# A six-product offset convolution in a deformable-convolution kernel, with the next image's tables begun one band earlier

## The chip, the cores and the metric

One NeuronCore of a Trainium2 chip runs the whole program. The metric is device time in microseconds (us). The kernel before took 1505.65 us, the median of three runs.

## The reference

Two layers work on eight images of 128 channels by 64 by 64 pixels, all float32. In layer 0 each image is group-normalised (32 groups), a 3x3 convolution makes 27 offset-and-mask maps from it, and a deformable 3x3 convolution samples the normalised image at those offsets. Its output is batch-normalised over all images, passed through a relu and added to the input. Layer 1 group-normalises the result and adds a mixture of four 3x3 convolutions (the two best per image, weighted) and a shared one.

```python
om = conv(gn(x), off_w, 3x3, pad 1) + off_b          # 27 maps: 9 (dy, dx) pairs, 9 masks
py, px = row + dy + ky - 1, column + dx + kx - 1      # for each of 9 taps
val = bilinear(gn(x), py, px) * sigmoid(mask)
y = einsum('bckhw,ock->bohw', val, w) + b
x = x + relu(batchnorm(y) * gamma + beta)
x = x + sum_e w_e * conv_e(gn(x)) + conv_shared(gn(x)) + biases
```

## The kernel before, in words

Layer 0 is the function `dense` and takes the first 1127.6 us of the profile; layer 1 takes the rest. `dense` is written with a manual schedule: every engine executes its instructions in the order in which the Python code emits them. So the order of the code is the order of each queue.

The work is cut into 64 **bands**, eight for each image, of eight image rows each. Band `g` belongs to image `b` and has the place `j` (0 to 7) in it. For each band the main loop emits, in this order:

- five **samples** (`sample`, line 714): matmuls of transposed pixels `xt` with bilinear weights `s` into the PSUM tile `pq` (three buffers). ScalarE moves each `pq` into `samples` (line 724). VectorE makes the `s` (`weights`, line 698) three samples ahead, from two weight tables `xwts` and `ywts`.
- nine **taps** of the deformable convolution of the band before (`conv`, line 763) into `py` (one PSUM buffer), which ScalarE moves out as `y` (line 771). In band 0 of an image the taps number eighteen, because the last band of the image before is cut into two pieces.
- among the taps: four groups of transposes `pt` (line 672) which ScalarE copies out as `xt` (line 677), the absolute values and clamps of `xwts` (lines 648 on ScalarE, 650 on VectorE), and copies of the pixels of a later band (`picked`, line 657).

`pt`, and every other PSUM tile of the offset work (`pm`, `pv`, `pc`), share **one** PSUM buffer (pool `ps_c`). A matmul into one of them waits until the one before it has been read.

The **tables** of an image are its bilinear weights. They are made from its offset convolution by a generator `tables(b)`, which `tick()` advances by one `yield` several times after each tap; `pause(n)` is n empty yields, so it sets how many ticks later the next piece is emitted. A `yield BLOCK` holds the generator until a tap whose number is in `BLOCKS`. The tables of image b+2 are begun in band 7 of image b and finished in band 5 of image b+1, just ahead of the first `load_x` for image b+2. The steps for one image are:

1. `statistics` (line 294): eight `bn_stats` on VectorE and one aggregate `mv`; six of them are emitted in band 6, the last two and the aggregate in band 7.
2. `pm` and `pv` (lines 309, 319): two one-column matmuls that average over a group's channels, in band 7 after the third and fourth tap. VectorE makes `d`, `e`, `gm` between them and `ve` after; GpSimd raises `ve` to the power -1/2 (`scale`, line 325), and VectorE makes `shift`.
3. The normalisation in place of `pad` in eight chunks, four on ScalarE (line 332) and four on VectorE (line 336).
4. The offset convolution. It takes rows in pairs: four **products** j = 0 to 3, each over half the rows. VectorE makes the row combinations `combo` (`combine`, line 360, two instructions of 128x1024 each), TensorE multiplies (`tap`, line 379: 3 column taps by 4 row groups of 32 PSUM partitions, 512 columns each), and VectorE adds the product into `om` (lines 408 to 415; ScalarE starts `om` at line 402).
5. ScalarE turns `om` (line 422), SyncE's queue writes it to DRAM (`rowwise`, `colwise`, lines 427 and 432) and reads it back with pixels on the partitions (lines 465 and 452). VectorE prepares distances from it (lines 503 to 518), the x table is stored (line 483), ScalarE makes five `tent`s of two instructions each (lines 537 and 541), VectorE multiplies each by the mask (line 574), and the y table is stored (line 564).

GpSimd's queue loads the tables: each band emits `load_x` for three bands ahead (line 632, two DMAs) and `load_y` for two bands ahead (line 617, eight DMAs). Image quarters are loaded by SyncE's queue in bands 2 to 5 (`load_quarter`, line 272).

## Time and profile before

| what | us |
|---|---|
| median of 3 runs (1500.36 to 1507.43) | 1505.65 |
| the profiled execution | 1504.96 |
| its span | 1503.2 |
| TensorE busy in the span | 1363.5 |
| VectorE busy | 959.3 |
| ScalarE busy | 818.3 |
| GpSimd busy | 449.9 |
| images 0 to 7 of layer 0, each from its first sample to the next image's | 147.5, 129.7, 133.2, 129.5, 129.3, 136.2, 128.2, 123.6 |

The image times count from the first sample matmul of band 0 of one image to that of the next, in the trace; image 0 starts at 70.5 us, and image 7 ends with the last tap of the deformable convolution at 1127.6 us. Image 7 makes no tables, so its bands show what a band costs without them.

### The profile page before, as it was taken

How to read it: one execution, taken by the hardware profiler on the slowest of the kernel's cores; microseconds unless marked ns; L12 is line 12 of the kernel's file. 1: busy time of each engine (PE TensorE's matmuls, PEld its weight loads, DVE VectorE, ACT ScalarE, POOL GpSimd, SP SyncE). 2: the span in 40 equal slices, each digit the busy share in tenths (PEclk: the TensorE clock that was granted, in tenths of full speed). 3: DMA queues.
4: the chain of work that ended last, by engine and by line, in shares of the span. 5: the costliest groups of instructions: out<-in, count | busy, mean ns of one | idle time of the engine just before them, and what ended most of it. 6: DMA issues, size and time to landing. Idle time of an engine off the chain costs nothing.

```text
span 1503.2 us, 21231 instructions
## 1 busy us (share of the span) xinstructions
PE 1363.5 (91%) x7714; PEld 761.6 (51%) x7714; DVE 959.3 (64%) x1906; ACT 818.3 (54%) x1095; POOL 449.9 (30%) x745
## 2 busy tenths in 40 slices
PE   4279799999999999999999899999994999999998
PEld 1245465556555555555556555566551444444443
DVE  5555475576557657656764775554528887888882
ACT  2365674776577468658656865866634232322320
POOL 6333242443334244333423333343303010110100
PEclk9589899999999999999999999999996999999999
DMA  4486775986697498669748866788708345665411
GB/s 143 115 181 126 175 163 105 213 190 137 128 202 179 95 196 214 137 130 207 187 99 183 194 147 135 168 183 200 171 26 248 93 124 149 168 168 154 110 45 58
DMA packets 130939, 227.27 MB, mean 151 GB/s; under 512 B 82003, under 2 KB 88303, under 8 KB 122137
## 3 DMA queue, kind: packets, MB, share of 16 engines
q0 software_dynamic: 54960, 137.08, 43.9%
q1 hardware_dynamic: 74848, 88.25, 19.9%
q8 instruction: 63, 1.03, 0.3%
q10 hardware_dynamic: 1017, 0.50, 0.1%
q14 instruction: 51, 0.42, 0.1%
HBM read 180.23 MB, written 45.35 MB: 150 GB/s over the span
## 4 chain that ended last, share of the span: by engine, by line
PE 53%; DMA 12%; ACT 9%; issue 9%; DVE 7%; SPq 2%; POOL 1%; ACTq 0%; DVEq 0%; POOLq 0%
PE py L763 20%; PE pc L1414 12%; PE pq L714 11%; PE pc L379 5%; PE pt L672 4%; DMA xwts<-tabx 4%; DMA pad<-in_x_dram 2%; ACT xwts L648 2%; ACT xt L677 2%; DMA combo<-colwise 2%; ACT work L537 1%; DMA x<-in_x_dram 1%; DMA yd<-y 1%; ACT samples L724 1%; DMA combo<-rowwise 1%
## 5 line engine op out<-in xcount | busy, mean ns | idle before, releaser
L763 PE MATMUL py<-samples,dw_sb 128*128 128x512 f32 (+3 forms) x1296 | 577.3, 562 | 7.1 <-ACT y L771 5.3
L617 POOL DMA_DIRECT2D ywts<-taby x504 | 305.5, 624 | 279.6 <-DMA xwts<-tabx 228.3
L714 PE MATMUL pq<-s,xt 64*128 64x144 f32 (+1 forms) x3840 | 283.8, 301 | 35.8 <-DVE s L698 24.7
L714 PEld LDWEIGHTS pq<-s,xt 64*128 64x128 f32 x3840 | 257.6, 190 | 84.7 <-ACT samples L724 24.2
L724 ACT COPY samples<-pq 128x864 f32<-128x864 f32 (+1 forms) x320 | 280.7, 974 | 33.6 <-PE pq L714 33.3
L763 PEld LDWEIGHTS py<-samples,dw_sb 128*128 128x128 f32 x1296 | 217.1, 190 | 160.3 <-issue 133.3
L677 ACT COPY xt<-pt 128x512 f32<-128x512 f32 (+1 forms) x256 | 142.4, 556 | 209.7 <-PE pt L672 209.2
L698 DVE TENSOR_TENSOR s<-xwts,ywts 128x72 f32<-128x72 f32 (+1 forms) x447 | 199.4, 499 | 84.6 <-PE pq L714 43.6
L650 DVE TENSOR_SCALAR xwts<-xwts 128x1152 f32<-128x1152 f32 (+2 forms) x130 | 97.3, 749 | 186.6 <-ACT xwts L648 186.2
L672 PEld LDWEIGHTS pt<-ident,picked 128*128 128x128 f32 x960 | 110.9, 141 | 171.7 <-ACT xt L677 105.0
L1414 PE MATMUL pc<-v,u 128*128 128x512 f32 x384 | 175.8, 605 | 6.3 <-DVE v L1321 6.3
L672 PE MATMUL pt<-ident,picked 128*128 128x128 f32 x960 | 152.8, 279 | 29.6 <-ACT xt L677 27.1
L632 POOL DMA_DIRECT2D xwts<-tabx x128 | 72.8, 573 | 353.5 <-DVE s L698 276.8
L1414 PE MATMUL pc<-v,wmix 128*128 128x512 f32 x384 | 174.0, 598 | 0.0
L648 ACT ACTIVATE xwts<-xwts,place 128x1152 f32<-128x1152 f32 (+2 forms) x130 | 160.9, 1242 | 11.5 <-DMA xwts<-tabx 11.5
L1392 ACT ACTIVATE t<-pc,bmix 128x512 f32<-128x512 f32 x32 | 22.0, 687 | 189.2 <-PE pc L1414 100.5
L1414 PEld LDWEIGHTS pc<-v,u 128*128 128x128 f32 x384 | 72.7, 192 | 93.5 <-issue 84.7
L1414 PEld LDWEIGHTS pc<-v,wmix 128*128 128x128 f32 x384 | 72.3, 190 | 91.4 <-issue 89.6
L360 DVE TENSOR_TENSOR combo<-pad 128x1024 f32<-128x1024 f32 x61 | 73.3, 1229 | 23.0 <-PE pc L379 14.4
L657 DVE COPY picked<-pad 128x960 f32<-128x960 f32 x128 | 81.9, 681 | 0.0
L771 ACT ACTIVATE y<-py,db_sb 128x512 f32<-128x512 f32 (+3 forms) x72 | 45.7, 635 | 65.6 <-PE py L763 31.1
L837 DVE BATCH_NORM_STATS2 ystats<-y 128x6 f32<-128x512 f32 (+3 forms) x72 | 44.5, 626 | 21.0 <-ACT y L771 21.0
(173 smaller groups left out, 955.3 us busy)
## 6 DMA issues: line engine op xcount, KB each, us to landing
xwts<-tabx POOLq DMA_DIRECT2D x128, 576.0 KB, 7.6
ywts<-taby POOLq DMA_DIRECT2D x504, 90.0 KB, 8.1
pad<-in_x_dram SPq DMA_DIRECT2D x36, 512.0 KB
out_dram<-yo SPq DMA_DIRECT2D x32, 512.0 KB
yd<-y SPq DMA_DIRECT2D x48, 256.0 KB
pad<-yd SPq DMA_DIRECT2D x16, 512.0 KB
x<-yd SPq DMA_DIRECT2D x16, 512.0 KB
x<-in_x_dram POOLq DMA_DIRECT2D x16, 512.0 KB, 9.2
```

The source lines that it names most:

```text
L379: nc.tensor.matmul(pcs[j][32 * q : 32 * q + 32].rearrange("p (h w) -> p h w", w=W)[:, :, lo:hi], lhsT=weight_of[j][:, kx], rhs=combo_of[j] ...
L617: engine.dma_start(out=y_wts[g % 2][at : at + NR * Q, r].rearrange("p a b c -> p (a b c)"), in_=bass.AP(tensor=y_table[b].tensor, offset=y ...
L648: nc.scalar.activation(part, part, AF.Abs, bias=column)
L650: nc.vector.tensor_scalar(part, part, -1.0, 0.0, ALU.add, ALU.min)
L657: nc.vector.tensor_copy(picked[g % 2][:, :, h], bass.AP(tensor=one.tensor, offset=one.offset, ap=[list(one.ap[0]), [T, NCOL], [W, Q], [1, Q]],
L672: nc.tensor.transpose(pt[:, c], picked[g % 2][:, c0 + c].rearrange("p h y x -> p (h y x)"), ident,)
L677: nc.scalar.copy(xts[g][:, c0 : c0 + n], pt[:, 0:n])
L698: engine.tensor_tensor(s[:, :, 3 * at : 3 * (at + k)].rearrange("p m (c x) -> p m c x", x=3), by_x[:, :, c : c + k], by_y[:, :, w : w + k] ...
L714: nc.tensor.matmul(by_m[:, h, :, at : at + k], lhsT=xts[g][rows, c], rhs=s[rows, :, at : at + k], start=True, stop=True,)
L724: nc.scalar.copy(bass.AP(tensor=one.tensor, offset=one.offset + first, ap=[list(one.ap[0]), [M * PLANE, 2], [PLANE, M], [WB + 1, 3], [1, w ...
L763: nc.tensor.matmul(py, lhsT=dw_sb[:, 3 * (2 - yy) + 2 - xx], rhs=samples[g % 2][:, m : m + 3 * n - 2 : 3, xx, 1 : W + 1], start=(i == 0), ...
L1414: nc.tensor.matmul(pc, lhsT=us[j][:, kx], rhs=vs[g][:, rows, kx : kx + W], start=(kx == 0), stop=(kx == 2),)
```

## The change

From the third image on (b = 2 to 7) the offset convolution takes rows in fours instead of pairs, with **six** products over a quarter of the rows each in place of four over half of them. Two products of 256 columns each go into one PSUM tile (`pair`), so there are three blocks in place of four. The row combinations are `combine_pair` (four VectorE instructions for each of three pairs); ScalarE moves every product from PSUM into SBUF, and VectorE combines them there (`mix`). The six weight sets are made once, in band 5 of image 0 (`quad_weights`).

The order moves too. All eight `bn_stats` are emitted in band 6, two after each of four taps, and `pm` and `pv` follow the eighth and ninth tap of band 6 (`BLOCKS` gets an 8). A tick at the very start of band 7 emits the power on GpSimd before that band's loads. Pauses before `shift`, before the combinations and after the loads of `om` change. Four small tiles of layer 1 get one buffer instead of two.

```diff
@@ tables(b) @@
                 ve = small.tile([P, 1], F32, name="ve")
+                if b > 1:
+                    yield
                 nc.vector.tensor_scalar(ve, pv[:, 0:1], GN_EPS, None, ALU.add)
-                yield from pause(3)
+                yield from pause(3 if b < 2 else 1)
                 scale = small.tile([P, 1], F32, name="scale")
                 nc.gpsimd.tensor_tensor(scale, ve, nhalf, ALU.pow)
-                yield from pause(8)
+                yield from pause(8 if b < 2 else 4)
...
+                def mix(out, a, times, c):
+                    if times in (1, -1):
+                        op = ALU.add if times == 1 else ALU.subtract
+                        nc.vector.tensor_tensor(out, c, a, op)
+                    else:
+                        nc.vector.scalar_tensor_tensor(out, a, float(times), c, ALU.mult, ALU.add)
+                def combine_pair(n):
+                    lo, hi = halves[n % 2]
+                    for args in (
+                        ((lo, row(2), -4, row(4)), (hi, row(1), -4, row(3)),
+                         (lo, hi, 1, lo), (hi, hi, -2, lo)),
+                        ((lo, row(2), -1, row(4)), (hi, row(1), -1, row(3)),
+                         (lo, hi, 2, lo), (hi, hi, -4, lo)),
+                        ((lo, row(2), -1.25, row(0)), (lo, row(4), 0.25, lo),
+                         (hi, row(3), -5, row(5)), (hi, row(1), 4, hi)),
+                    )[n]:
+                        mix(*args)
+                        yield from pause(PACE[n])
+                def pair(n):
+                    yield BLOCK
+                    pc = ps_c.tile([P, CH], F32, name="pc", tag="pc")
+                    for i, j in enumerate(((1, 2), (3, 4), (0, 5))[n]):
+                        weight = quad_of[j]
+                        for kx in (1, 0, 2):
+                            lo, hi = max(0, 1 - kx), min(W, W + 1 - kx)
+                            for q in range(4):
+                                nc.tensor.matmul(
+                                    pc[32 * q : 32 * q + 32, CH // 2 * i : CH // 2 * (i + 1)]
+                                    .rearrange("p (h w) -> p h w", w=W)[:, :, lo:hi],
+                                    lhsT=weight[:, kx],
+                                    rhs=halves[n % 2][i][
+                                        :, 4 * q : 4 * q + 4, lo + kx - 1 : hi + kx - 1],
+                                    start=(kx == 1), stop=(kx == 2), skip_group_check=True)
+                    pcs[n] = pc.rearrange("p (i t w) -> p i t w", i=2, w=W)
+                    yield from pause(2)
+                if b < 2:
...
+                else:
+                    yield from pause(11)
+                    yield from combine_pair(0)
+                    yield from combine_pair(1)
+                    yield from pair(0)
+                    nc.scalar.activation(quad[:, 0], pcs[0][:, 0], AF.Identity, bias=offb_sb)
+                    nc.scalar.copy(quad[:, 1], pcs[0][:, 1])
+                    yield from pause(4)
+                    mix(quad[:, 0], quad[:, 1], 1, quad[:, 0])
+                    mix(quad[:, 1], quad[:, 1], -2, quad[:, 0])
+                    yield from combine_pair(2)
+                    yield from pair(1)
+                    nc.scalar.copy(quad[:, 2:4], pcs[1])
+                    yield
+                    yield from pair(2)
+                    ends = om[:, 1, 0:CH].rearrange("p (i t w) -> p i t w", i=2, w=W)
+                    nc.scalar.copy(ends, pcs[2])
+                    for at, a, times, c in (
+                        (2, 3, 1, 2), (3, 3, -2, 2),
+                        (0, 2, 1, 0), (2, 2, 3, 0), (1, 3, 2, 1), (3, 3, 6, 1),
+                    ):
+                        mix(quad[:, at], quad[:, a], times, quad[:, c])
+                    mix(quad[:, 0], ends[:, 0], 1, quad[:, 0])
+                    mix(quad[:, 3], ends[:, 1], 1, quad[:, 3])
+                    yield
...
-                yield from pause(50)
+                yield from pause(50 if b < 2 else 57)
@@ main loop @@
-            PIXELS, BLOCKS, SPREAD = (0, 1, 5, 6), (2, 3, 4, 7), (1, 3, 5, 7)
+            PIXELS, BLOCKS, SPREAD = (0, 1, 5, 6), (2, 3, 4, 7, 8), (1, 3, 5, 7)
+            def quad_weights():
+                v0, v1, v2, v3, v4, v5 = quad_of
+                nc.vector.tensor_tensor(v2, v0, v5, ALU.add)
+                nc.vector.tensor_tensor(v1, v2, v3, ALU.add)
+                nc.vector.tensor_tensor(v2, v2, v3, ALU.subtract)
+                nc.vector.scalar_tensor_tensor(v4, v5, 4.0, v0, ALU.mult, ALU.add)
+                nc.vector.scalar_tensor_tensor(v3, v3, 2.0, v4, ALU.mult, ALU.add)
+                nc.vector.scalar_tensor_tensor(v4, v4, 2.0, v3, ALU.mult, ALU.subtract)
+                for v, n in ((v1, -6.0), (v2, -6.0), (v3, 24.0), (v4, 24.0)):
+                    nc.scalar.activation(v, v, AF.Copy, scale=1.0 / n)
...
                 turned = pixels(g + 1) if g + 1 < len(bands) else iter(())
+                if j == NB - 1:
+                    tick()
...
-                    if odd == 0 and (j == NB - 2 and part < 6 or j == NB - 1 and part < 2):
-                        next(means_of, None)
-                    if odd == 0 and j == NB - 1 and part == 2 and b + 2 < B:
+                    if odd == 0 and j == NB - 2 and part in (0, 1, 2, 4):
+                        for _ in range(2):
+                            next(means_of, None)
+                    if odd == 0 and j == NB - 2 and part == 7 and b + 2 < B:
                         made = tables(b + 2)
                         next(made)
...
+                if g == 5:
+                    quad_weights()
```

The tiles `yscale`, `yshift`, `tot` and `mb` of layer 1 change from two buffers to one (`bufs=1`).

More of the change, by code (lines that the diff above doesn't have):

```diff
@@ L199, in dense @@
             offu_sb = [a1.tile([P, 3, 32], F32, name=f"offu_sb{i}") for i in range(2)]
+            offv_sb = a1.tile([P, 3, 32], F32, name="offv_sb")
+            quad_of = (
+                offw_sb[:, 0:3], offu_sb[0], offu_sb[1], offw_sb[:, 3:6], offv_sb, offw_sb[:, 6:9]
+            )
             offb_sb = a1.tile([P, 1], F32, name="offb_sb")
@@ L397, in block @@
                     yield from pause(2)
-                for j in (1, 2):
-                    yield from combine(j)
-                yield from block(1)
-                nc.scalar.activation(even, taken(1), AF.Identity, bias=offb_sb)
-                yield from combine(0)
-                yield from block(2)
-                if b == 0:
-                    yield from combine(3)
-                m2 = taken(2)
-                nc.vector.tensor_tensor(odd, even, m2, ALU.subtract)
-                nc.vector.tensor_tensor(even, even, m2, ALU.add)
@@ L410, in tables, with row @@
-                if b:
-                    yield from combine(3)
-                yield from block(0)
-                nc.vector.tensor_tensor(even, even, taken(0), ALU.add)
-                yield from block(3)
-                nc.vector.tensor_tensor(odd, odd, taken(3), ALU.subtract)
-                yield
+                PACE = 2, 2, 2
+                quad = omr.rearrange("p (t i w) -> p i t w", i=4, w=W)
+                halves = [(t[:, 0 : H // 4], t[:, H // 4 :]) for t in combos]
+                def row(k):
+                    return pad[:, ROWPAD - 1 + k :][:, 0 : H - 3 : 4]
@@ new lines, in mix @@
+                def mix(out, a, times, c):
[7 more added lines that the diff above has]
+                    for args in (
+                        (
+                            (lo, row(2), -4, row(4)), (hi, row(1), -4, row(3)),
+                            (lo, hi, 1, lo), (hi, hi, -2, lo),
+                        ),
+                        (
+                            (lo, row(2), -1, row(4)), (hi, row(1), -1, row(3)),
+                            (lo, hi, 2, lo), (hi, hi, -4, lo),
+                        ),
+                        (
+                            (lo, row(2), -1.25, row(0)), (lo, row(4), 0.25, lo),
+                            (hi, row(3), -5, row(5)), (hi, row(1), 4, hi),
+                        ),
+                    )[n]:
+                        mix(*args)
+                        yield from pause(PACE[n])
@@ new lines, in pair @@
+                def pair(n):
[11 more added lines that the diff above has]
+                                    rhs=halves[n % 2][i][
+                                        :, 4 * q : 4 * q + 4, lo + kx - 1 : hi + kx - 1
+                                    ],
+                                    start=(kx == 1), stop=(kx == 2),
+                                    skip_group_check=True,
+                                )
+                    pcs[n] = pc.rearrange("p (i t w) -> p i t w", i=2, w=W)
+                    yield from pause(2)
@@ new lines, in tables @@
+                if b < 2:
+                    for j in (1, 2):
+                        yield from combine(j)
+                    yield from block(1)
+                    nc.scalar.activation(even, taken(1), AF.Identity, bias=offb_sb)
+                    yield from combine(0)
+                    yield from block(2)
+                    if b == 0:
+                        yield from combine(3)
+                    m2 = taken(2)
+                    nc.vector.tensor_tensor(odd, even, m2, ALU.subtract)
+                    nc.vector.tensor_tensor(even, even, m2, ALU.add)
+                    if b:
+                        yield from combine(3)
+                    yield from block(0)
+                    nc.vector.tensor_tensor(even, even, taken(0), ALU.add)
+                    yield from block(3)
+                    nc.vector.tensor_tensor(odd, odd, taken(3), ALU.subtract)
+                    yield
[23 more added lines that the diff above has]
+                    mix(quad[:, 3], ends[:, 1], 1, quad[:, 3])
+                    yield
@@ L1134, in layer1 @@
     def layer1():
-        yscale = small.tile([P, 1], F32, name="yscale")
+        yscale = small.tile([P, 1], F32, name="yscale", bufs=1)
         rsqrt(yscale, ymv[:, 1:2], BN_EPS)
         nc.vector.tensor_tensor(yscale, yscale, gamma_sb, ALU.mult)
-        yshift = small.tile([P, 1], F32, name="yshift")
+        yshift = small.tile([P, 1], F32, name="yshift", bufs=1)
         nc.vector.tensor_tensor(yshift, ymv[:, 0:1], yscale, ALU.mult)
@@ L1299, in prepare @@
                 )
-                tot = small.tile([P, 1], F32, name="tot")
+                tot = small.tile([P, 1], F32, name="tot", bufs=1)
                 nc.vector.tensor_reduce(tot, wd, AX.X, ALU.add)
@@ L1306, in mix_biases @@
                 def mix_biases():
-                    mb = small.tile([P, NE], F32, name="mb")
+                    mb = small.tile([P, NE], F32, name="mb", bufs=1)
                     nc.vector.tensor_tensor(mb, eb_sb, wd, ALU.mult)
```

## The prediction, made before the changed kernel ran

> **What bounds the kernel now.** I read the page first (busy times, then the chain that ended last), then the table by stretches with one stretch for each band of image 3, then TensorE's timeline inside those bands.

> ```profile
> PE 1363.5 (91%) x7714; PEld 761.6 (51%) x7714; DVE 959.3 (64%) x1906; ACT 818.3 (54%) x1095; POOL 449.9 (30%) x745
> ```

> ```profile
> 480.80:500.90 20.10, 18.41 (x136) 12.54 (x135) 14.58 (x25) 13.12 (x18) 5.82 (x10) 1.00 0.58 118
> 500.90:523.10 22.20, 21.99 (x166) 10.55 (x165) 13.31 (x25) 9.32 (x13) 5.64 (x10) 1.00 0.44 93
> 523.10:537.20 14.10, 14.10 (x94) 8.57 (x93) 8.61 (x18) 10.98 (x14) 6.19 (x10) 1.00 0.82 173
> ...
> 565.20:581.10 15.90, 14.47 (x95) 8.57 (x94) 10.18 (x21) 15.47 (x24) 5.71 (x9) 1.00 0.81 193
> 581.10:595.00 13.90, 13.90 (x94) 8.50 (x93) 11.95 (x24) 9.98 (x14) 7.02 (x10) 1.00 0.99 241
> 595.00:610.30 15.30, 14.63 (x98) 8.83 (x97) 9.31 (x24) 9.69 (x13) 7.17 (x13) 1.00 0.78 179
> ```

> The columns are stretch, length, then busy us (count) of PE, PEld, DVE, ACT and POOL. TensorE is busy 14.0 of 14.0 us in a plain band: it is the bound, at full clock. Image 7 makes no tables; its bands 0 and 1 take 15.9 and 13.6. So an image costs 15.9 + 13.6 + 6 x 14.0 = 113.5 without tables, and image 3, at 129.5, pays 16.0 for them: bands 0, 1, 5 and 7 hold it. What stands in them is this:

> ```profile
> 638.09 2.83 PE L379 MATMUL pc<-combo,offu_sb 128*32 128x512 f32 x24
> 613.88 1.93 PE L714 MATMUL pq<-s,xt 64*128 64x144 f32 x24 [0.93 <-ACT samples L724]
> 568.50 1.93 PE L714 MATMUL pq<-s,xt 64*128 64x144 f32 x24 [0.66 <-ACT samples L724]
> 578.87 0.55 PE L672 MATMUL pt<-ident,picked 128*128 128x128 f32 x3 [0.77 <-ACT xt L677]
> 603.69 0.35 PE L309 MATMUL pm<-mv,gsel 128*128 128x1 f32 x2 [0.67 <-DVE mv L297]
> ```

> One product takes about 2.75 us, four take 11.0. The rest are waits: 0.93 in band 0 (ScalarE late by three normalisations of 0.7), 0.66 and 0.77 in band 5 (ScalarE late by the tents), 0.67 in band 7 (VectorE's statistics). In the same view images 2 and 5 lose 2.95 and 4.51 more in band 5 waiting for `s`, whose tables came late, and image 2 2.12 at `pm`; that is why they take 133.2 and 136.2.

> [...]

> **The change, part by part** (one image, unless said).

> *Products.* 512 columns cost 423 ns a round of four, so 256 should cost about 212 (the transposes, 128 columns, follow at 108 ns each: time goes with columns). [...] A product of six rounds: 1.27; six: 7.6, and 0.15 to begin each of three blocks: 8.1. From 11.0 this is **-2.9**. No row shows 256 columns in four tiles. Lower bound 7.6; upper bound: if each record were paced by its own weight load (110 ns in the L379 rows), 144 x 0.110 = 15.8.

> *VectorE.* Combinations: 8 x 1.22 (L360) become 12 of the same size; the fused kind costs the same an element (1415 ns for 1152 on L1342), so 12 x 1.23 = 14.8. Into `om`: 4 x 0.69 become 10 of 256 columns at about 0.42 (0.56 for 384 on L1353, 0.23 for 72 on L698): 4.2. Together +6.4 us. I count it as nothing because bands 7 to 1 leave VectorE 6.0, 5.5 and 8.9 us idle (table above). By hand, band 7: `s` done at 6.8, `shift` and three chunks 8.4, clamp (after ScalarE) 9.6, chunk and pixels 11.3, second clamp at 14.1, one combination to 15.3, that is 0.9 into band 0; the next `s` is done at 1.5 and wanted at 2.55. Band 0 to 1: the last combination ends 1.6 into band 1, `s` at 2.15, again in time.

> *ScalarE.* One 0.69 becomes two of 256 and two of 512 columns, about 2.2 us. Its four normalisations move from the end of bands 7 and 0 to the middle of band 7, ahead of the third `xt`: first clamp half ends at 8.9, four chunks x 0.71 to 11.7, `xt` 12.2, and the transpose wanted at 11.75 waits 0.5. In exchange band 0's 0.93 goes. In band 1 both turns of `om` (L422, 0.9 each) and an `xt` precede `y`, which is read 1.8 into band 2; the fourth sample waits about 0.3.

> *Band 5.* With pause(57), two tents stand before band 4's `y` where one stood, and three stand between the second and third `xt` where two stood there and one earlier. A tent is 1.39 (0.80 + 0.59, start to start). So the first wait grows to 0.66 + 1.39 = 2.05. The second: second `xt` done 9.65, clamp half to 10.85, three tents to 15.0, third `xt` 15.5, transpose wanted at 13.9: 1.7. Band 5 becomes 14.0 + 3.75 = 17.7, **+1.8**.

> *Statistics.* In band 6 VectorE: `s` done at 5.9 (image 3 had 7.6, held by the `ywts` landing, but band 6 now starts 1.8 later against the loads), eight statistics x 0.60, a clamp 0.7 and the aggregate end at 11.8; pixels and second clamp 13.7, `d` and `e` 14.0. TensorE wants `pm` at 13.0, but the one PSUM buffer is free only when the fourth `xt` is done, 13.25; then a tap, and `pv` at 14.5: `e` is there. Band 6 grows to 14.8 (**+0.9**), band 7 falls from 15.3 to 14.4 (**-0.9**). If `s` stays at 7.6, `pv` waits 1.7 more: both ends go into the range. What queues behind a late `pv` is all of band 7 on TensorE.

> *Power.* It moves past the ten load issues of band 7 on GpSimd's queue and those now stand behind it, waiting for `ve`. In the before they began 2.9 into the band, waiting for `s`; `ve` comes within 0.2 of its start and the power takes 0.65. Nothing.

> *SyncE.* `rowwise` and `colwise` are issued some 4 to 6 us earlier against the bands (`om` is final 16 us into band 1, not at its end), and the reads back now stand ahead of the first quarter load, not behind it. The x table then lands before band 5's `load_x` in images 2 and 5 too: **-3.7** and **-6.7**, nothing in the others.

> *Image 1* works at four ticks a tap: six combinations fall into band 7 of image 0, `s` is late by 2.5 in band 0, and a tent more stands before a third `xt`: in sum 129.2 for 129.7. *Weights*: six small VectorE and four ScalarE operations, once, about 0.6. *Layer 1*: the smaller pools hold tiles that VectorE makes and reads in order: nothing.

> **The sum.** Image 3 by band (0 to 7): 18.6 (15.9 + 2.7), 19.2 (13.6 + 5.4 + 0.2), 14.3, 14.0, 14.0, 17.7, 14.8, 14.4: 127.0 for 129.5. Image 0 +0.6, 1 -0.5, 2 -6.2, 3 -2.5, 4 -2.3, 5 -9.2, 6 -2.4: together -22.5. The profiled execution took 1504.96, so 1482.5; the median of the runs is 0.7 above it. I predict **1483**.

> **The rivals.**
> *A: the waits go too.* If the tents find ScalarE free earlier than my hand schedule has it, band 5 stays at 15.9 or better and band 7's 0.5 goes: 6 x 1.8 + 5 x 0.9, about 15 more: 1467, at best 1450. For it: ScalarE has 4 us a band to spare outside band 5. Against: its order is fixed, and image 1, which had two tents ahead of `y`, waited 2.34 there.
> *B: the gain is eaten.* The late tables of images 2 and 5 come back (+10.4), and `pv` waits 1.7 in five images (+8.5): 1502. For it: the SyncE reads of L465 and L452 are on the chain with 14.6 and 10.2 us. Against: they start earlier.
> *C, slower: the products are paced by weight loads.* Each record costs 110 ns instead of 53: 15.8 an image, 7.7 above my 8.1: 1483 + 6 x 7.7 = 1529. It decides from about 78 ns a record, where 6 x 144 x 0.025 us takes back the 22. For it: a 512-column product already shows one record every 112 ns, as long as one load, and I cannot tell from that row alone which sets it. Against: the loads start 25 to 33 ns apart, and samples (144 columns, two row halves) run a record every 69 ns though their loads last 186.

> **How the numbers follow.** Forecast 0.56, A 0.20, B 0.16, C 0.08. The measurement can tell 0.5%, 7.5 us: faster means below 1498. Faster: nearly all of the forecast and A, a third of B: 0.80. Same: the rest of B and a little of the forecast: 0.13. Slower: C, less its mild end: 0.07. The range runs from 1460 (inside A) to 1503 (the end of B) and leaves out C and the best of A.

> **What would show it.** Right: the product rows near 1.35 us for 24 records; image times near 127 with no wait for `s` in band 5; band 5 near 17.7, waiting for `samples` and `xt`; `pm` and `pv` in band 6 without a wait above 0.5. Wrong: product records 100 ns apart (C); a wait of TensorE for `s` at the start of bands 0 or 1 (VectorE overfull); a wait at `pv` above 1 us (B); a band 5 of 16 or less (A).

## The result, and the profile after

The changed kernel took 1488.95 us, the median of six runs (1487.48 to 1493.12), where the kernel before took 1507.90 beside it (six runs, 1500.36 to 1516.48). The ratio is 0.9889, with a 95% interval of 0.9859 to 0.9918: 12 to 21 us faster. The forecast was 1483 with a range of 1460 to 1503. The profiled execution took 1488.83 with a span of 1487.1, that is 16.1 less than the span before.

Image by image, counted as before:

| image | 0 | 1 | 2 | 3 | 4 | 5 | 6 | 7 |
|---|---|---|---|---|---|---|---|---|
| before | 147.5 | 129.7 | 133.2 | 129.5 | 129.3 | 136.2 | 128.2 | 123.6 |
| after | 148.0 | 132.0 | 127.7 | 129.0 | 127.3 | 128.9 | 126.1 | 123.6 |
| predicted difference | +0.6 | -0.5 | -6.2 | -2.5 | -2.3 | -9.2 | -2.4 | 0 |
| measured difference | +0.5 | +2.3 | -5.5 | -0.5 | -2.0 | -7.3 | -2.1 | 0 |

The busy times of the page after:

```profile
PE 1347.2 (91%) x8002; PEld 773.0 (52%) x8002; DVE 995.2 (67%) x1972; ACT 827.4 (56%) x1117; POOL 445.1 (30%) x745
```

The same table by stretches as before, for bands 0, 1, 2, 5, 6 and 7 of image 3 (stretch, length, busy us and count of PE, PEld, DVE, ACT and POOL, then PEclk, DMA share and GB/s):

```profile
477.70:496.70 19.00, 18.24 (x160) 13.28 (x159) 16.17 (x25) 10.76 (x15) 5.67 (x10) 1.00 0.57 125
496.70:515.60 18.90, 18.90 (x190) 11.19 (x189) 15.38 (x31) 10.96 (x15) 5.61 (x10) 1.00 0.55 123
515.60:530.00 14.40, 14.24 (x94) 8.57 (x93) 8.49 (x18) 10.51 (x15) 5.12 (x9) 1.00 0.80 141
...
558.00:577.70 19.70, 16.05 (x96) 9.37 (x95) 11.35 (x22) 16.26 (x24) 6.18 (x11) 0.91 0.85 178
577.70:592.30 14.60, 14.50 (x100) 8.99 (x99) 12.20 (x27) 9.54 (x13) 6.27 (x10) 1.00 0.86 217
592.30:606.70 14.40, 14.11 (x94) 8.43 (x93) 9.54 (x22) 12.15 (x16) 6.84 (x11) 1.00 0.69 159
```

Bands 0 and 1 became 1.1 and 3.3 us shorter and band 7 0.9 shorter; band 6 grew by 0.7 and band 2 by 0.3. Band 5 went from 15.9 to 19.7, and in the column PEclk (the clock that TensorE was granted, 1.00 being full speed) it has what no line of mine had allowed for: 0.91. In image 2 the same band has the same work and full clock, and is 1.6 shorter:

```profile
430.20:448.30 18.10, 14.45 (x96) 8.59 (x95) 11.35 (x22) 16.15 (x24) 6.34 (x11) 1.00 0.87 175
```

TensorE's timeline shows the new products and what is waited for:

```profile
223.46 1.87 PE L806 MATMUL pq<-s,xt 64*128 64x144 f32 x24 [2.83 <-DVE s L790]
...
434.83 1.93 PE L806 MATMUL pq<-s,xt 64*128 64x144 f32 x24 [2.03 <-ACT samples L816]
446.05 0.55 PE L764 MATMUL pt<-ident,picked 128*128 128x128 f32 x3 [1.62 <-ACT xt L769]
...
492.51 2.77 PE L452 MATMUL pc<-combo,offu_sb 128*32 128x256 f32 x48
562.61 2.58 PE L806 MATMUL pq<-s,xt 64*128 64x144 f32 x24 [2.03 <-ACT samples L816]
```

The line at 492.51 is a pair of products: 48 records in 2.77 us, where 24 records of twice the width took 2.83. In its records the second round of four matmuls begins 240 ns after the first, each later one 212 to 216 ns after the one before. The four weight loads of a round begin 6 to 7 ns apart and last 106 to 110 ns each. The two waits at 434.83 and 446.05 are those of band 5, forecast at 2.05 and 1.7. The lines at 434.83 and 562.61 are the same 24 matmuls after the same wait, in image 2 and in image 3; the second takes 2.58 for 1.93. The clock records have TensorE at half speed from 563.7 for 3.41 us, and likewise from 307.7 (image 1) and 819.7 (image 5). I call these half-clock stretches.

### The profile page after: what moved, and what is told of

Same layout as the page of the kernel before. It is cut to its first block, busy times and chain, and to the rows that moved or that the text cites. A ratio compares the mean times of both kernels' runs of the same rounds, so it can differ in the third digit from the quotient of the medians.

```text
span 1487.1 us, 21850 instructions
## 1 busy us (share of the span) xinstructions
PE 1347.2 (91%) x8002; PEld 773.0 (52%) x8002; DVE 995.2 (67%) x1972; ACT 827.4 (56%) x1117; POOL 445.1 (30%) x745
## 4 chain that ended last, share of the span: by engine, by line
PE 51%; issue 9%; ACT 8%; DMA 5%; DVE 3%; POOL 1%; ACTq 0%; POOLq 0%; SPq 0%; DVEq 0%
PE py L855 20%; PE pq L806 12%; PE pc L1523 11%; PE pt L764 5%; PE pc L452 3%; DMA pad<-in_x_dram 2%; ACT xwts L740 2%; DMA x<-in_x_dram 1%; ACT xt L769 1%; ACT pad L339 1%; ACT work L629 1%; ACT work L633 1%; ACT om L514 1%; ACT y L863 1%; ACT samples L816 1%
## 5 line engine op out<-in xcount | busy, mean ns | idle before, releaser
L709 POOL DMA_DIRECT2D ywts<-taby x504 | 299.6, 611 | 298.5 <-DMA xwts<-tabx 241.1
L724 POOL DMA_DIRECT2D xwts<-tabx x128 | 73.3, 577 | 317.8 <-DVE s L790 265.2
L666 DVE TENSOR_TENSOR work<-work,combo 64x576 f32<-64x576 f32 x40 | 29.5, 746 | 39.3 <-ACT work L633 39.3
```

The lines of the kernel that those rows point to most:

```text
L709: engine.dma_start(out=y_wts[g % 2][at : at + NR * Q, r].rearrange("p a b c -> p (a b c)"), in_=bass.AP(tensor=y_table[b].tensor, offset=y ...
L724: engine.dma_start(out=x_wts[g % 3][HALF * h : HALF * h + HALF], in_=bass.AP(tensor=x_table[b].tensor, offset=x_table[b].offset + (2 * j + ...
```

## The experiments

My theory after the result: products, statistics and the moved SyncE work did what the working said, and what was missing (7.9 us of the images) lay in image 1's layout and in half-clock stretches that the waits of band 5 set off. From there the question became what those waits were worth. Each time stands beside runs of the kernel before on the same chip; its medians there lay between 1503.5 and 1511.1. The new kernel was not run again beside them, so where two versions differ by a few us, the argument rests on the band times in their traces and not on the medians. Three chips were used.

**e1: the new order with the old products.** `if b < 2` became true for every image, with pause(11) ahead of the combinations as in the six-product path. From image 2 on its products take weight sets made for the six-product form, so its offsets have other values; the instructions are those of four products.

> The new order of the statistics, pv, power and tables with the old four products of 512 columns in every image. The theory says that six images get back 2.9 us of products each and lose the tables that came late, so 1489 + 6 x 2.9 = 1506 at most; the new kernel's own half-clock stretches (1.6 us each) stay where its band-5 waits stay. So 1500 to 1507, with image 2 near 130 and image 5 near 131, not 133 and 136. A rival, that the order alone brings the gain and the products nothing: 1489 to 1492. A second rival, that the order is worth nothing without the products: 1508 and an s wait of 3 to 4.5 us again in band 5 of images 2 and 5.

Measured: 1498.09 (ratio 0.9917, 0.9888 to 0.9945), 2 below the forecast's lower end. Images 2 to 6 took 131.1, 129.5, 129.5, 129.5 and 128.3: in images 2 and 5 TensorE no longer waits for `s` in band 5, so **the order of the tables alone removes these waits**, and the two rivals fall. The first line is the kernel before, the second e1, both in band 5 of image 5:

```profile
831.65 3.11 PE L714 MATMUL pq<-s,xt 64*128 64x144 f32 x24 [4.51 <-DVE s L698]
```

```profile
830.52 1.92 PE L807 MATMUL pq<-s,xt 64*128 64x144 f32 x24 [1.90 <-ACT samples L817]
```

Bands 0 to 2 of image 3 take 21.9 + 19.5 + 14.0 = 55.4, against 52.3 with six products: the products are worth 3.1 an image, forecast 2.9. Image 1 gains nothing from them: its bands 0 and 1 take 41.0 us here and 41.1 in the new kernel. The total is only 9 above the new kernel, for two reasons. In images 3 to 6 band 5 is 17.1 here without a half-clock stretch, 1.0 shorter than with six products (waits of 1.90 and 0.77 for 2.03 and 1.62): a tent half falls between the third and fourth `xt` of band 4 and another tent between the first and second of band 5. And this run has two half-clock stretches in images 1 to 6 where the new kernel has three. Against that, image 0 took 3.1 more, which I did not follow up.

**e2: image 1 laid out as the later images.**

```diff
-                    for _ in range(3 + (g < NB) if twice == 1 else 1 + done % 2):
+                    for _ in range(3 + (g < NB - 1) if twice == 1 else 1 + done % 2):
```

> The tables of image 2 advance three ticks a tap in band 7 of image 0 as in the bands of later images (not four). Theory: image 1's loss is its own layout, six combinations in two bands and two turns; laid out as in later images it has no s wait of 2.8 us in band 0 and one product pair less there, so image 1 goes from 132.0 to 127.3 to 129 (the upper end with a half-clock stretch of 1.6 in band 5), and the kernel from 1489 to 1485 to 1486. Rival, that image 1 is late because VectorE is behind from image 0: 1489, image 1 at 132 still, the s wait still there.

Measured: 1489.17. Image 1 went from 132.0 to 129.1 and its `s` wait of 2.83 is gone, so its layout was the cause of these. The total did not move: this run has half-clock stretches in band 5 of images 1, 2, 4 and 5, one more than the new kernel, and image 0 took 149.5 for 148.0. By the total alone e2 would say nothing.

**e3 and e7: filling the wait.** Matmuls of `ident` by `ident` (128 columns) that nothing reads, ahead of the fourth sample of band 5 in images 1 to 6; fifteen in e3, seven in e7.

```diff
+                        if j == NB - 3 and q == 3 and 1 <= b < B - 1:
+                            pf = ps_c.tile([P, CH], F32, name="pf", tag="pc")
+                            for _ in range(7):
+                                nc.tensor.matmul(pf[:, 0:P], lhsT=ident, rhs=ident, start=True, stop=True)
                         sample(g * NGR + q)
```

> Fifteen matmuls of 128 columns (about 1.6 us at full clock, nothing reads them) stand ahead of the fourth sample of band 5 in images 1 to 6, in TensorE's wait of 2.03 us. Theory, that the clock falls to half after such a wait: with the wait filled, band 5 of images 3 and 5 goes from 19.7 to about 18.1, image 1's band 5 from 18.1 to 16.5, and images 2, 4 and 6 keep 18.1; the kernel is 3 to 5 us faster, 1484 to 1486. Rival, that the clock falls at these places for another reason (a fixed time, the load): bands 5 stay at 19.7 and the kernel at 1489. Should the filler itself run late it would add up to 1.6 an image: 1498.

e3 measured: 1493.08, slower. The fifteen took 3.62 us. My estimate of 1.6 was 15 times the 108 ns at which I had seen transposes of 128 columns follow each other, but the timeline has 30 records for the fifteen: each of these matmuls has two, which I had counted as one. That is 1.6 more than the wait, and band 5 grew to 19.5 in images 2 to 6, as the last sentence of its expectation allows, though no half-clock stretch was left in images 1 to 6. So the size was mended:

> Seven matmuls in the wait in place of fifteen (e3 showed 15 taking 3.62 us, twice what was meant, so 7 take 1.7). Theory: no half-clock stretch in band 5 of images 1 to 6, band 5 at 18.1 in all of images 2 to 6 and at 16.5 in image 1; 1484 to 1485.5, against 1489. Rival, that a wait is not what sets the clock: 19.7 in two or more of these bands, 1488 to 1490.

e7 measured: 1485.43 (1484.88 to 1486.68). Band 5 is 18.1 in images 2 to 6 and 16.6 in image 1, and there is no half-clock stretch between 189 and 1113 us. Band 5 of image 3, by stretches:

```profile
556.50:574.60 18.10, 16.20 (x110) 10.22 (x109) 11.35 (x22) 16.19 (x24) 6.30 (x11) 1.00 0.85 185
```

TensorE does 1.75 us more in this band than in image 2 of the new kernel (14.45) and the band is as long: the filler lies in the wait. It is 1.6 shorter than the same band of the new kernel. With the wait left in, three of six images had the stretch in the new kernel, four in e2 and four in e6; with it filled, none of six in e3 and none in e7. **The wait set off the half clock**; that part of the loss was 3 times 1.6, and layer 0 of e7 ends 4.6 us earlier than in the new kernel.

**e4: the tents six ticks earlier.** `pause(57)` became `pause(51)`.

> pause(57) becomes pause(51): two tents still stand before band 4's y, but only one and a half between second and third xt in band 5, the rest moves to band 4's middle. Theory: the samples wait of 2.03 stays, the xt wait of 1.62 goes (2.1 us of tents fit in the 2.2 that ScalarE idles there), at most 0.3 is added at band 4's fourth xt; band 5 goes from 18.1 to 16.6, six images by 1.3 to 1.6: 1479 to 1482. Rival, that the earlier VectorE work makes s late, or the data are not there: a DVE wait in band 5 takes the place, 1488 or more.

Measured: 1485.74, spread from 1476.87 to 1488.87. Band 5 fell to 15.7 (14.4 in image 1), further than the theory's 16.6: the `xt` wait went, and the `samples` wait, which was to stay at 2.03, fell to 1.52. But in the profiled run (1488.87, the slowest of the four) band 6 of images 1, 4 and 5 grew to 18.3, 16.9 and 18.8, and band 7 to 16.1, 17.4 and 16.2 with half-clock stretches in it (PEclk 0.82 in band 7 of image 4). The rival, late data, was right in kind, but it had put the wait into band 5. VectorE's timeline, in band 6 of images 1, 4 and 5:

```profile
327.06 1.80 DVE L790 TENSOR_TENSOR s<-xwts,ywts 128x432 f32<-128x432 f32 x4 [4.89 <-DMA xwts<-tabx]
...
706.52 1.80 DVE L790 TENSOR_TENSOR s<-xwts,ywts 128x432 f32<-128x432 f32 x4 [3.22 <-DMA ywts<-taby]
...
838.67 1.79 DVE L790 TENSOR_TENSOR s<-xwts,ywts 128x432 f32<-128x432 f32 x4 [5.10 <-DMA xwts<-tabx]
```

and what TensorE made of it in image 1:

```profile
334.83 0.35 PE L314 MATMUL pm<-mv,gsel 128*128 128x1 f32 x2 [2.88 <-DVE mv L302]
```

The `s` waited for tables to land, the eight statistics stood behind it, and `pm` behind them. The view names `ywts` in image 4 and `xwts` in images 1 and 5. I read all three as the `ywts` of band 7, which are issued in band 5; the `xwts` of that band were issued a band earlier. GpSimd's timeline in band 5 of image 4 shows the loads:

```profile
687.71 1.29 POOL L724 DMA_DIRECT2D xwts<-tabx  x2 [3.11 <-DVE s L790]
688.99 3.46 POOL L709 DMA_DIRECT2D ywts<-taby  x6
695.37 1.04 POOL L709 DMA_DIRECT2D ywts<-taby  x1 [2.92 <-DMA xwts<-tabx]
698.32 0.59 POOL L709 DMA_DIRECT2D ywts<-taby  x1 [1.91 <-DMA xwts<-tabx]
```

The two `xwts` loads, for three bands on, go first; of the eight `ywts` loads, for two bands on, the last two wait until the `xwts` have landed. In the new kernel the last two wait likewise (1.09 and 2.50 us in the same band), but band 5 was 2.4 to 4.0 us longer and `pm` did not wait in band 6. Two explanations remained: full DMA engines, or the order of this queue.

**e5 and e6: image quarters a band earlier**, to take traffic out of band 5 (`1 <= j < 5` and `j - 1` in place of `2 <= j < 6` and `j - 2`); e5 with e4's pause, e6 with the new kernel's. The last quarter then replaces rows of band 7 before its pixels are copied, so band 7 samples pixels of another image; the amount of work is the same.

> The tents six ticks earlier, as in e4, and the four image quarters loaded in bands 1 to 4 in place of 2 to 5. Theory: what took e4's gain back was the weight tables of band 7 landing too late for VectorE's s of band 6 (waits of 3.2 to 5.1 us in images 1, 4 and 5), because the loads of bands 4 to 6 fill the DMA engines (1.05 and 0.85 of them in image 3 of the new kernel); with the quarter out of band 5 those waits go, pm in band 6 does not wait, images 1 to 6 take 125.0 each (image 1: 129.5) and the kernel 1475 to 1479, with the runs close together. Rival, that the landing is set by the order of the loads on GpSimd's queue and not by the traffic: band 6 waits as in e4, 1485 to 1489.

> The new kernel with only the quarters moved from bands 2 to 5 to bands 1 to 4. Theory: in the new kernel the long band 5 hides the landing, so nothing is gained where pm did not wait: 1486 to 1490, bands 5 at 18.1 or 19.7 as before. Rival, that DMA traffic is what makes band 5 and image 1 long: 1480 or less.

e5 measured: 1490.18, e6: 1499.40 (ratio 0.9973). In e5 the waits of band 6 shrank (bands 6 of 16.8, 14.6, 15.5, 14.6 and 15.7 in images 1 to 5) without going, so traffic may have a share; but image 0 took 155.7 and 155.4 us for 148.0, as its band 5 grew to 33.8 and 32.3. In e6 TensorE waits 11.5 us for `s` there, in the new kernel 6.0, and the x table of image 1 is stored at 176.3 us for 168.8; that the moved quarters delay it is likely but was not isolated. This is a worse place for the quarters, and no decision between the two explanations. e6 missed its forecast of 1486 to 1490: 7.4 of the miss are image 0, and four of its bands 5 have a half-clock stretch. Its rival (1480 or less) falls.

**e9: `load_y` ahead of `load_x`**, on e4:

```diff
-                        if q == 2:
-                            load_x(g + 3, nc.gpsimd)
                         if q in (2, 3):
                             for k in range(T * (q - 2), T * (q - 1)):
                                 load_y(g + 2, k, nc.gpsimd)
+                        if q == 3:
+                            load_x(g + 3, nc.gpsimd)
```

> e4 (tents six ticks earlier), and on GpSimd's queue each band issues its eight load_y before its two load_x instead of after. In band 5 load_x waits for the x table of the next image to be stored, and the eight load_y for band 7 of the same image stand behind it. Theory: the landing that took e4's gain back is late for that order; with it gone there is no wait for xwts or ywts in band 6 of images 1 to 6, images 2 to 5 take 125.0, image 6 123.8, image 1 129 and the kernel 1474 to 1478. Rival, that the DMA engines are full in bands 4 to 6 and the order doesn't matter: waits of 3 to 5 us in band 6 of some images, 1483 to 1489.

Measured: 1471.61 (1468.57 to 1473.79; ratio 0.9785, 0.9729 to 0.9840), below the forecast. Images 2 to 5 take 125.0 each, image 1 127.7, band 6 is 14.6 in images 1 to 5, and no half-clock stretch is left between 189 and 1097 us. GpSimd's timeline in band 5 of image 4:

```profile
680.79 4.69 POOL L709 DMA_DIRECT2D ywts<-taby  x8 [6.88 <-DVE s L790]
685.42 1.15 POOL L724 DMA_DIRECT2D xwts<-tabx  x2
```

All eight go in 4.69 us with no wait among them. **The order of the queue was what kept e4's gain back**, and the rival of full DMA engines falls as the main cause: bands 5 and 6 of image 4 move 218 and 212 GB/s here, where e4 moved 202 and 192.

**e8 and e10: tents between the samples.** Both put three of the five tents between the sample copies of band 5 by calls of `tick` in the sample loop, both lay image 1 out as e2. e8 keeps each multiplication by the mask behind its tent and has the quarters of e5 (with the same note on its pixels); e10 puts the five multiplications after the tents and has the loads of e9.

> Quarters a band earlier, image 1 laid out as the later ones, and the tents laid where ScalarE is idle: the first in the middle of band 4, three between the samples of band 5 (five ticks after each of its first, third and fourth sample), the last between first and second xt. Theory: ScalarE's order is all that band 5 waits for; both waits (3.65 us) and with them the half-clock stretches go, band 5 takes 14.0 to 14.7, images 1 to 5 take 123.3 to 124.5, image 6 122 and the kernel 1459 to 1468. Rival, that the tents now hold the sample copies (three tents and five copies are 9.1 us in a sample phase of 9.65) or that the loads become the bound: band 5 at 16 or waits for ywts in band 6, 1472 to 1480.

> e8 mended: three tents of ScalarE stand between the samples of band 5, but VectorE's five multiplications by the mask come after all tents, in the tap phase, so that no s stands behind them; load_y ahead of load_x as in e9; image 1 as the later ones; the quarters where the new kernel has them. Theory: e8's 3.2 us in band 5 were s behind a multiplication that waited for a tent; now band 5 takes 14.0 to 14.7, images 1 to 5 take 123.4 to 124.2, image 6 122.5, image 0 148 to 150: 1460 to 1467. Rival, that the loads cannot follow at this pace: waits for ywts or xwts of 2 to 4 us in band 6, 1472 to 1482.

e8 measured 1488.89, e10 1489.60. Both lie more than 20 us above their forecasts. 10.3 us of e8 are image 0, which took 158.3 for 148.0, with the quarters moved as in e5 and e6; in e10 image 0 took 148.4. In e8 band 5 is 17.7 in images 1 to 6. The first line is TensorE's in image 3, the second VectorE's just before it:

```profile
567.58 1.13 PE L806 MATMUL pq<-s,xt 64*128 64x144 f32 x12 [1.71 <-DVE s L790]
```

```profile
566.16 0.75 DVE L666 TENSOR_TENSOR work<-work,combo 64x576 f32<-64x576 f32 x1 [2.21 <-ACT work L633]
```

A multiplication that waits for a tent stands ahead of the `s`. Another 1.6 us are a wait for `xt` (in all but image 5). e10 took the multiplication away, and ScalarE itself was late: band 5 takes 18.3 in image 4 and 20.0 in the five others, which have a half-clock stretch each (in image 3, eight tap matmuls at 568.95 take 5.33 us, those at 584.50 in the next band 3.67). What e8's rival said, that the tents hold the sample copies, is what e10 shows. TensorE in image 3 of e10:

```profile
562.05 1.13 PE L808 MATMUL pq<-s,xt 64*128 64x144 f32 x12 [1.09 <-ACT samples L818]
...
568.45 0.66 PE L766 MATMUL pt<-ident,picked 128*128 128x128 f32 x4 [2.88 <-ACT xt L771]
```

The error was a reading: I took the sample phase for 5 x 1.93 = 9.65 us, but the line of 1.93 holds two samples. All five take 4.2, and ScalarE's five copies take 4.4: it has no free time there. Its free time lies among the taps. In the new kernel, the five samples of band 6 and the five copies of band 4, image 3:

```profile
577.67 4.21 PE L806 MATMUL pq<-s,xt 64*128 64x216 f32 x60
```

```profile
545.21 4.36 ACT L816 COPY samples<-pq 128x1008 f32<-128x1008 f32 x5 [0.38 <-PE pq L806]
```

**e11 and e12: tents on VectorE.** e9, image 1 as in e2, and one or two of the five tents made by VectorE with the three instructions that image 0 already uses (`other_tent`). The core of e12:

```diff
-                    for i in range(NR):
-                        yield from tent(i)
-                        yield from pause(2)
+                    for i in (0, 3, 1, 4, 2):
+                        if i > 2:
+                            other_tent(i)
+                        else:
+                            yield from tent(i)
+                            yield from pause(2)
                         masked(i)
-                        yield from pause(2)
+                        yield from pause(12 if i == 0 else 0 if i > 2 else 2)
```

> e9 with image 1 laid out as the later images and one of the five tents (i = 3) made by VectorE in three instructions instead of ScalarE in two, in the tap phase. e10 fell because I took the sample phase for 9.65 us; it is 4.2, and ScalarE's five copies fill it, so ScalarE's idle time lies among the taps. Theory: one tent of 1.39 less ahead of band 4's y takes the samples wait of band 5 from 1.5 to about 0.7: six images by 0.8, image 1 by 2.4 more by its layout: 1463 to 1466. Rival, that VectorE (11.1 us busy in band 5 of e9, 12.1 in band 6) is late with s or with the statistics: no gain in band 5 or pm waiting in band 6, 1469 to 1473.

> As e11 with two tents (i = 3 and 4) on VectorE; none stands ahead of band 4's y but the second half of the first. Theory: no wait for samples is left in band 5, band 5 takes 14.0 to 14.3, images 2 to 5 take 123.5: 1459 to 1462. Rival, that VectorE's two tents (some 3 us with its 11.1 fill a band of 14) make s or the statistics of band 6 late: band 6 or 7 grow by 1 to 3 us an image, 1466 to 1478, slower than e11.

e11 measured 1463.63 (1460.08 to 1466.48; ratio 0.9708, 0.9670 to 0.9745), e12 **1459.23** (1455.25 to 1461.38; ratio 0.9678, 0.9640 to 0.9715), both inside their forecasts. In e11 the `samples` wait of band 5 fell from 1.52 to 0.14 (forecast 0.7). Bands 5 and 6 of image 3 in e12, by stretches:

```profile
546.00:559.90 13.90, 13.90 (x94) 8.46 (x93) 11.82 (x25) 12.09 (x16) 5.64 (x10) 1.00 0.83 200
559.90:574.80 14.90, 14.80 (x100) 9.12 (x99) 14.24 (x31) 9.56 (x13) 5.78 (x10) 1.00 0.83 204
```

Band 5 is a plain band: TensorE has no wait in it. VectorE is busy 14.24 of 14.90 us in band 6, so there is little room for more of it. Images 2 to 5 take 123.3 to 123.4, against 113.5 without tables; e12 is the best version of this study, 30 us below the new kernel. Layer 0 of e12 ends 12.8 us earlier than that of e9; 4.1 of these are image 1 with the layout of e2, and the rest is mainly band 5.

## Why the prediction was right, and where it missed

The direction and its main terms held. By step:

- **Products.** Forecast -2.9, measured -3.1 in bands 0 to 2 between e1 and the new kernel. A round of four begins every 212 to 216 ns, where I had 212, so a record costs 53 to 54 ns for the 53 forecast; with the ends of a block it is 2.77 us for 48 records, 58 ns each. The 78 ns from which rival C decides are far off, and C is refuted. One reading of mine was wrong although nothing came of it: I took the starts of a product's first four loads, 25 to 33 ns apart in the kernel before (at 638.09), for the time of a load. The same four last 106 to 109 ns each, and in the new rows loads start 6 to 7 ns apart and last 106 to 110 ns. The four of a round overlap, and the rounds keep their pace of 212 to 216 ns.
- **VectorE's extra 6.4 us, at no cost.** In images 2 to 6 no `s` wait appeared in bands 0, 1 or 2, as the working by hand had it; the 0.67 left in band 0 is a wait for `y` that the kernel before has too. In image 1 the `s` wait was 2.83 against 2.5.
- **ScalarE.** The 0.93 of band 0 went. The wait in band 7 was 0.29 for 0.5, that of the fourth sample in band 2 0.16 for 0.3.
- **Band 5.** The two waits came as 2.03 and 1.62 for 2.05 and 1.7. The band was 18.1 for 17.7, as TensorE's own work in it takes 14.45, not 14.0. The table in my prediction already had 14.47 there, and I added the waits to a plain band instead. Images 2 to 6 by 0.4 make 2.0 of the miss.
- **Statistics and bands 6, 7.** 14.6 and 14.4 for 14.8 and 14.4 in image 3; `pm` and `pv` do not wait. The rival B case (a `pv` late by 1.7) did not come in the new kernel. In e4, as soon as band 5 was short, its mechanism came, `s` held by the landing, and `pm` waited 1.2 to 3.1 us.
- **Late tables.** -3.7 and -6.7 in images 2 and 5: gone, as e1 shows by the order alone.
- **The step that failed** is band 5 taken as work plus waits at full clock. A wait of 2.0 us is not only 2.0 us: in three of six images it was followed by 3.41 us at half clock, 1.6 more each, 4.8 in all. Band 5 of image 5 before (21.3 us long with 5.3 idle, so 16.0 busy for 14.4) already had such a stretch, of 3.41 us from 832.1: in the line at 831.65 above, 24 matmuls take 3.11 us that take 1.93 elsewhere. I had put all of it down to the late table.
- **Image 1** was forecast at -0.5 and came at +2.3: 1.6 of the difference is its half-clock stretch. For the other 1.2 the forecast gave only a sum, so no single term of it can be blamed. Against the kernel before, bands 0 and 1 together are 1.6 shorter, band 6 is 0.7 longer and band 4 is 1.7 longer, most of it this wait:

```profile
300.58 0.55 PE L764 MATMUL pt<-ident,picked 128*128 128x128 f32 x3 [1.32 <-ACT xt L769]
```

So 4.8 + 2.0 + 1.2 make up, but for rounding, the 7.9 us that images 0 to 6 fell short by. The span fell 1.5 more than the images show, 1.2 of it in layer 1 (375.6 to 374.4), where I had forecast nothing and ran nothing. Both kernels are at half clock for 23.89 us at the start of layer 1 and again at its end; between these the kernel before has a stretch of 3.41 us (at 1176.8) and the new one has none. Over the fourteen traces layer 1 takes 375.1 to 377.5 us in the five with such a stretch and 373.9 to 375.3 in the nine without, so the 1.2 cannot be put down to the change. Rival A (the waits go too) was not what the change did, but e9 and e12 show what it was worth: 1471.6 with 1.5 of the 3.65 us of waits left, 1459.2 with them gone and image 1 laid out anew, where I had put A at 1467 and its best at 1450.

## What to carry to other kernels

A wait on the engine that sets the time can hide a lateness behind it: e4 took 2.4 us out of band 5 and in its profiled execution lost all of it again to a load queue whose order had cost nothing until then. So before shortening a stage, look at which transfers land just inside it and what stands ahead of them in their queue. In a queue shared by two loads, the one that is needed sooner goes first, above all where the other waits for something (e4 to e9: 1485.74 to 1471.61 us). And read free time from the phase in which you want to use it: ScalarE had 4 us a band to spare, but none of it in the 4.2 us where e8 and e10 put the work.

## What the runs showed of the hardware

| idle in a full-clock window | windows | followed by half clock |
|---|---|---|
| 1.98 to 2.98 us | 20 | 20 |
| 1.62 to 1.95 | 37 | 4 |
| under 1.62 | 3443 | 1 |

In all 20 windows with 1.98 us or more idle, half clock followed; of the 37 between 1.62 and 1.95 it followed in 4, so there the idle time alone does not decide it. In the kernel before, one of these windows has 2.98 us idle (from 828.7) and the next most idle has 1.65; in the new kernel three have 2.30, 2.03 and 2.03 (from 304.3, 560.3 and 816.3) and the next has 1.79. Half clock followed these four and, in this stretch of the two traces, no others. In the new kernel the wait of 2.03 in image 3 (560.58 to 562.61) lies wholly in the window from 560.3 to 563.7; in image 2 (432.80 to 434.83) the grid line at 434.0 cuts it into 1.21 and 0.82, and the clock stayed at 1.00. So images with equal work differ by 1.6 us, and e2, which moved the later bands against the grid, paid in other images. Filling such a wait with unread matmuls (e7) gained 3.5 us by the medians; removing it gained more.
